# P^T of an attention head rests in DRAM for one head more

## The chip, the core and the metric

The kernel runs on one core of a Trainium2 chip. The core has five engines that work side by side, each with its own queue in order: TensorE (PE; its weight loads are shown apart as PEld), VectorE (DVE), ScalarE (ACT), GpSimd (POOL) and SyncE (SP), which issues all of this kernel's DMAs. The metric is the device time of one execution in microseconds (us). One execution is recorded instruction by instruction: that is the profile.

## The reference

Two transformer layers over 2 batches of 512 rows of 512, all in float32, cut here to what matters:

```python
x = x + layernorm(L0_attn(layernorm(x)))   # 32 heads of 128, 8 of K and V, RoPE, causal
x = x + layernorm(L0_ffn(layernorm(x)))    # one linear layer with LoRA
x = x + layernorm(L1_attn(layernorm(x)))   # 32 heads, RMS norm of q and k, biases, not causal
x = x + layernorm(L1_ffn(layernorm(x)))    # silu(x w1) * (x w3), then w2, with LoRA
# attention: softmax(q k^T / sqrt(128)) v, then a product with Wo
```

Per head the softmax gives a 512 x 512 matrix P. TensorE needs it transposed, P^T, to form O^T = V^T P^T ("P V").

## The kernel before

**Products.** Each float32 operand is split into hi + lo[...], and a product is three matmuls: hi hi, hi lo and lo hi (`mm3`, L393). So most results are read twice: a cast makes hi (ACT, or DVE), a subtraction lo (POOL, or DVE).

**Units and heads.** A unit is two heads of one batch; layer 0 has units 0 to 31, layer 1 units 32 to 63. A head (n, j) is head j of unit n. A unit has projections (q, k, v), scores, softmax, P V and the output projection with Wo (`out_proj`, `post(n)`), which adds to the accumulator y.

**P^T.** In most units ("lag", L1446: units 2 to 26 and 33 to 62) P is transposed in two steps (`softmax_tail`, L681): DVE transposes 32 x 32 blocks into a tile T, a DMA stores T in a DRAM buffer (`pd` in layer 1, `pd0`, shown as pc, in layer 0; three of each, used in turn, L1534), and four DMAs load it back with the blocks in place into a tile PT, by halves of the queries. Then casts and subtractions make the hi and lo tiles "pt" from it, which `av_items` (L839) multiplies with V. In the other units TensorE does the transposes (`pv_items`, L767).

**Order of work.** The program is emitted by a generator on the host which keeps its own estimate of each engine's clock. TensorE's work is a list of items with conditions: a main list in the order of heads and "fills" (projections, output projections, P V), each with a nominal place in main. A fill is issued when its place has come, or earlier when main has to wait (`streams`, L345). The work of other engines follows in stages; a stage is a piece of a Python generator, and `yield` hands over until the time estimated for its work. Each engine then runs its queue in the order emitted. In `run` (L1535 on), the interval of head i holds the scores of head i + 1 and P V of head i - 1.

**Slots.** Large tiles lie in an arena of 37 slots of 4 KB per partition; a tile takes a half or the whole of one (`HALF`, L218). Each kind has a limit of its own, partly different for each of six phases of the work (`PHASES`, L40). Requests for a kind queue in order (`wait`, L325). Weights take W slots: Wq, Wk, Wv and Wo of a unit, or of a pair of units, two slots each in layer 1.

**Scores in layer 1** (`l1_score`, L1169). DVE takes the negative maximum m of each row of the scores from PSUM; a second DVE instruction multiplies m by the row's RMS factor r (mr = m r); ACT computes exp(r s + mr) with two pointer operands.

## Time and profile before

| | us |
|---|---|
| three runs | 2106.71, 2111.2, 2113.66 (median 2111.2) |
| span of the profiled execution | 2117.8 |
| idle of PE in 0 to 110, 590 to 800, 1910 to 2118 | 8.4, 6.0, 11.0 |
| P^T in layer 0 (pc) and layer 1 (pd): first store to last load | 58.0 to 618.6, 817.1 to 1874.0 |
| median from issue to landing: store of T in layer 1, a load of PT, a load of Wo | 3.7, 3.3, 3.6 |

The time of a run is that of the whole execution. The profiled execution is another one and its span is from the first to the last instruction; it is 6.6 us above the median of the runs. Its instructions all carry one line, L102, the helper which records them; they are told apart by their tiles. "ar" is any tile of the arena, "ps_oy" the PSUM bank of P V, of the output projection and of the last feed-forward product, "ps_s" that of the scores, "ps_pj" that of projections, "m", "mr" and "rq" the row values of the scores in layer 1. In a group line the figures are the total busy time, the mean of one instruction, and the engine's idle time just before them with what ended it. In a line of waits they are total, number and longest. In the timeline they are start, length, engine and instruction, with the idle time before it in brackets.

### The profile page before, as it was taken

The page shows a single profiled execution, that of the slowest core. Times are in us where ns is not written, and L with a number is a line of the kernel's source. Part 1 is how long each engine was busy: PE and PEld are TensorE (multiplying, and loading weights), DVE is VectorE, ACT ScalarE, POOL GpSimd, SP SyncE. Part 2 cuts the span into 40 slices and gives each one's busy share as a digit, 9 for nine tenths or more (in the row PEclk, how much of TensorE's full clock was granted, in tenths as well). Part 3 has the DMA queues.
Part 4 walks back from the last instruction along what each step waited for, and adds up shares of the span by engine and source line. Part 5 has one row for each costly group of instructions (what it writes and reads, how often), then busy time and mean ns, then how long its engine had stood idle before and what let it go on. Part 6 is the DMA issues. An engine that isn't in the chain of part 4 may idle for free.

```text
span 2117.8 us, 41211 instructions
## 1 busy us (share of the span) xinstructions
PE 2056.7 (97%) x12605; PEld 1827.5 (86%) x12605; DVE 1801.4 (85%) x4210; ACT 1337.7 (63%) x3247; POOL 1446.3 (68%) x1786
## 2 busy tenths in 40 slices
PE   8999999999999999999999999999999999989998
PEld 7888888888888798889899999999999898977886
DVE  7998899899888889889889999899989988888534
ACT  5776677577766668776666666666667666664212
POOL 5686678688875567877677777777777776774212
PEclk9999999999999999999999999999999999999999
DMA  2476567577652235887877777777777787763021
GB/s 98 127 183 166 145 185 183 143 200 199 177 159 66 71 103 166 244 232 223 227 202 229 220 227 211 207 221 219 225 206 232 213 240 212 224 178 93 31 67 44
DMA packets 476566, 370.54 MB, mean 175 GB/s; under 512 B 117400, under 2 KB 424488, under 8 KB 476344
## 3 DMA queue, kind: packets, MB, share of 16 engines
q1 hardware_dynamic: 476344, 367.91, 60.9%
q8 instruction: 99, 1.62, 0.3%
q14 instruction: 123, 1.01, 0.2%
HBM read 232.12 MB, written 135.66 MB: 174 GB/s over the span
## 4 chain that ended last, share of the span: by engine, by line
PE 54%; DMA 12%; DVE 9%; SPq 3%; issue 2%; POOL 2%; ACT 2%; DVEq 0%; ACTq 0%; POOLq 0%
PE ps_pj L102 23%; PE ps_oy L102 19%; PE ps_s L102 10%; DVE ar L102 6%; SPq L102 3%; DMA pd<-ar 3%; DMA ar<-pd 2%; POOL ar L102 2%; DMA kdk<-ar 2%; ACT ar L102 2%; DMA ar<-kdq 2%; DMA kdq<-ar 2%; PE ps_tr L102 1%; DMA ar<-pc 1%; DVE m L102 1%
## 5 line engine op out<-in xcount | busy, mean ns | idle before, releaser
L102 POOL TENSOR_TENSOR ar<-ar,ar 128x256 fp32r<-128x256 f32 (+4 forms) x1223 | 1058.3, 887 | 456.6 <-ACT ar L102 333.6
L102 PE MATMUL ps_oy<-ar,ar 128*128 128x256 f32 (+2 forms) x4014 | 832.2, 342 | 28.7 <-DVE ar L102 14.0
L102 PEld LDWEIGHTS ps_oy<-ar,ar 128*128 128x128 f32 x4014 | 653.5, 190 | 133.1 <-DVE ar L102 22.5
L102 ACT CAST ar<-ar 128x256 fp32r<-128x256 f32 (+3 forms) x1166 | 531.5, 490 | 305.4 <-DMA ar<-pd 117.1
L102 PE MATMUL ps_pj<-ar,xh 128*128 128x256 f32 (+1 forms) x3392 | 635.2, 285 | 0.9 <-POOL ar L102 0.6
L102 PEld LDWEIGHTS ps_pj<-ar,xh 128*128 128x128 f32 x3392 | 536.0, 190 | 14.5 <-POOL ar L102 1.1
L102 PE MATMUL ps_pj<-ar,xl 128*128 128x256 f32 (+1 forms) x1696 | 482.9, 285 | 0.0
L102 DVE STREAM_TRANSPOSE ar<-ar 128x256 f32<-128x256 f32 (+3 forms) x688 | 347.9, 533 | 16.9 <-DMA pd<-ar 9.7
L102 DVE TENSOR_TENSOR ar<-ps_pj,ar 128x512 f32<-128x512 f32 (+2 forms) x448 | 305.4, 683 | 52.5 <-PE ps_pj L102 44.8
L102 PE MATMUL ps_s<-ar,ar 128*128 128x512 f32 (+2 forms) x1252 | 338.5, 376 | 8.6 <-DVE ar L102 4.7
L102 PEld LDWEIGHTS ps_pj<-ar,xl 128*128 128x128 f32 x1696 | 322.9, 190 | 2.1 <-DVE xl L102 0.7
L102 PE MATMUL ps_pj<-xh,ar 128*128 128x512 f32 x816 | 286.6, 399 | 0.7 <-ACT xh L102 0.7
L102 DVE TENSOR_TENSOR y<-ps_oy,y 128x512 f32<-128x512 f32 x272 | 184.8, 680 | 81.8 <-PE ps_oy L102 80.2
L102 PEld LDWEIGHTS ps_s<-ar,ar 128*128 128x128 f32 x1252 | 214.5, 189 | 44.0 <-DVE ar L102 12.6
L102 DVE TENSOR_TENSOR ar<-ar,ar 128x256 fp32r<-128x256 f32 (+5 forms) x328 | 207.9, 652 | 51.1 <-ACT ar L102 50.1
L102 ACT ACTIVATE ar<-ps_s,mr,rq 128x512 f32<-128x512 f32 x256 | 198.6, 777 | 46.7 <-DVE mr L102 36.9
L102 PEld LDWEIGHTS ps_pj<-xh,ar 128*128 128x128 f32 x816 | 154.0, 189 | 31.7 <-ACT xh L102 1.1
L102 DVE TENSOR_REDUCE m<-ps_s 128x1 f32<-128x512 f32 x256 | 170.9, 673 | 6.2 <-PE ps_s L102 5.0
L102 ACT ACTIVATE ar<-ar,ri 128x512 f32<-128x512 f32 (+3 forms) x245 | 149.6, 621 | 38.3 <-DVE ri L102 37.1
L102 POOL TENSOR_SCALAR ar<-ar,ri 128x512 f32<-128x512 f32 (+3 forms) x202 | 133.0, 661 | 54.3 <-DVE ri L102 48.9
L102 PE MATMUL ps_pj<-xl,ar 128*128 128x512 f32 (+1 forms) x408 | 161.2, 395 | 0.0
L102 ACT ACTIVATE ar<-ps_s,m 128x512 f32<-128x512 f32 (+3 forms) x256 | 133.8, 526 | 23.4 <-DVE m L102 14.8
(91 smaller groups left out, 2105.5 us busy)
## 6 DMA issues: line engine op xcount, KB each, us to landing
pd<-ar SPq DMA_DIRECT2D x240, 256.0 KB, 3.7
ar<-pd SPq DMA_DIRECT2D x480, 128.0 KB, 3.3
ar<-pc SPq DMA_DIRECT2D x200, 128.0 KB, 3.0
ar<-in_wq SPq DMA_DIRECT2D x86, 256.0 KB, 4.1
ar<-in_wo SPq DMA_DIRECT2D x86, 256.0 KB, 3.6
kdk<-ar SPq DMA_DIRECT2D x31, 512.0 KB, 4.8
ar<-kdk SPq DMA_DIRECT2D x124, 128.0 KB, 4.0
kdq<-ar SPq DMA_DIRECT2D x31, 512.0 KB, 5.1
```

The costliest lines, as they stand in the source:

```text
L102: r = self.k.tc.keep_in_program_order(f(*args, **kw))
```

## The change

P V of a lagged head comes two heads behind its scores instead of one: the interval of head i holds P V of head i - 2. With it:

- five DRAM buffers instead of three; a head's store waits in the generator until the head five before it has issued its loads
- in layer 1 the loads, and after them the casts, are issued in the order of heads (`turn`)
- the output projection of a unit moves one head back, and its Wo and V stay that much longer
- tiles of the kinds W, v, nat and raw are given out only while two more slots are free
- the feed-forward weights of layer 1 wait until the last unit's Wo is in
- in layer 1's scores one instruction in place over PSUM multiplies by r and takes the minimum of the row (K carries a negative factor); exp then has the scale -1 and that minimum as its bias
- two stores of x are followed by a `yield` before the tile is released

Without the comments and docstrings that it drops, the diff is:

```diff
@@ room
         free = sum(not u for u in self.used)
+        if tag in ("W", "v", "nat", "raw"):
+            free -= 2
@@ setup
-        self.pd0 = [[...] for i in range(3)]
-        self.pd = [... for i in range(3)]
+        self.pd0 = [[...] for i in range(5)]
+        self.pd = [... for i in range(5)]
+        self.loads, self.turn, self.places = {}, [0, 0], 0
@@ consts
-        ...scalar_tensor_tensor(self.g, self.gqk[:, 0:1], SCALE, ...)
+        ...scalar_tensor_tensor(self.g, self.gqk[:, 0:1], -SCALE, ...)
@@ resid, after each store of x
+            yield
             self.rel(x)
@@ softmax_tail, before T
+        head = st["head", j]
+        while self.loads.get(head - 5, 2) < 2:
+            yield 0.1
+        self.loads.setdefault(head, 0)
@@ softmax_tail, before PT
+        o = 1 - h if st["causal"] else h
+        while not st["causal"] and self.turn[0] < st["place", j] + o:
+            yield 0.1
         yield from self.wait("PT")
+        self.turn[0] = max(self.turn[0], st["place", j] + o + 1)
         (the four loads)
+        self.loads[head] += 1
         yield
+        while not st["causal"] and self.turn[1] < 2 * head + o:
+            yield 0.1
@@ softmax_tail, in the loop over kc, and pv_items with its last transpose
+            if kc == ((0, 1)[h] if st["causal"] else NT - 1):
+                self.turn[1] = max(self.turn[1], 2 * head + o + 1)
@@ l1_score
-            m = self.t("m", [P, 1])
-            nc.vector.tensor_reduce(m, ps, AX.X, ALU.max, negate=True)
-            yield
             while "rq" not in st:
                 yield 0.3
             r = st["rq"][:, 2 * qt + j:2 * qt + j + 1]
-            mr = self.t("mr", [P, 1])
-            nc.vector.tensor_tensor(mr, m, r, ALU.mult)
-            yield
-            self.rel(m)
-            yield from self.softmax_tail(st, j, qt, ps, mr, r, S)
+            m = self.t("m", [P, 1])
+            nc.vector.tensor_scalar(ps, ps, r, 3.0e38, ALU.mult, ALU.min, accum_out=m)
+            yield
+            yield from self.softmax_tail(st, j, qt, ps, m, -1.0, S)
@@ f1_weights, first half of each weight
+                    while "o" not in self.wlast:
+                        yield 0.5
@@ run
+        self.vlast, self.wlast = pre(NA - 1)[2]["v"], wt(NA - 1, 0)
-            pre(n)[2]["slot", j] = i % 3
+            pre(n)[2]["slot", j] = i % 5
+            pre(n)[2]["head", j] = i
+            pre(n)[2]["place", j] = self.places
+            self.places += 2 * lag[n]
+        pend = []
@@ run, j == 0
+                if n > 1 and lag[n - 2] and lag[n - 1]:
+                    fill["o"] += post(n - 2)
@@ run, j == 1
-                if n > 0 and lag[n - 1]:
+                if n and lag[n - 1] and not lag[n]:
                     fill["o"] += post(n - 1)
@@ run, every head
-            if i and lag[heads[i - 1][0]]:
-                todo += av_lag(*heads[i - 1])
+            while pend and (len(pend) >= 2 or not lag[n]):
+                todo += av_lag(*heads[pend.pop(0)])
+            if lag[n]:
+                pend.append(i)
...
-                if L == 0 and i and lag[heads[i - 1][0]]:
+                if L == 0 and lag[n] and todo:
```

More of the change, by code (lines that the diff above doesn't have):

```diff
@@ L416, in setup @@
         self.used = [set() for _ in self.arena]
-        self.pd0 = [[self.dr.tile([P, 4, 2, 64 * (h + 1)], F32, name=f"pc{i}{h}") for h in range(2)] for i in range(3)]
-        self.pd = [self.dr.tile([P, 2, 4, 256], F32, name=f"pd{i}") for i in range(3)]
+        self.pd0 = [[self.dr.tile([P, 4, 2, 64 * (h + 1)], F32, name=f"pc{i}{h}") for h in range(2)] for i in range(5)]
+        self.pd = [self.dr.tile([P, 2, 4, 256], F32, name=f"pd{i}") for i in range(5)]
         self.kd = {n: [self.dr.tile([P, 4, 256], F32, name=f"kd{n}{i}") for i in range(2)] for n in "kq"}
         self.ready = {}
+        self.loads, self.turn, self.places = {}, [0, 0], 0
         self.ident = cp.tile([P, P], F32, name="ident")
@@ L434, in consts @@
         yield
-        nc.vector.scalar_tensor_tensor(self.g, self.gqk[:, 0:1], SCALE, self.gqk[:, 1:2], ALU.mult, ALU.mult)
+        nc.vector.scalar_tensor_tensor(self.g, self.gqk[:, 0:1], -SCALE, self.gqk[:, 1:2], ALU.mult, ALU.mult)
     def bcast(self, tile_, src):
@@ L778, in tr @@
                 self.rel(*[st["p", j, qt] for qt in range(NT)])
+                self.turn[1] = max(self.turn[1], 2 * st["head", j] + 2)
             n = S - q0 * P
@@ L1511, in run @@
         at(f - 1, 1, [self.l1_init])
-        self.vlast = pre(NA - 1)[2]["v"]
+        self.vlast, self.wlast = pre(NA - 1)[2]["v"], wt(NA - 1, 0)
         at(NA - 2, 0, self.f1_init())
@@ L1547, in run @@
                         fill["q"] += qk_mid(n + 1)
-                if lag[n]:
+                if lag[n] and 1:
                     fill["v"] += v_mid(n)
@@ L1553, in run @@
             else:
-                if n > 0 and lag[n - 1]:
+                if n and lag[n - 1] and not lag[n]:
                     fill["o"] += post(n - 1)
+                if lag[n] and 0:
+                    fill["v"] += v_mid(n)
                 if n + 1 < NA and lag[n] and not lag[n + 1]:
```

## The prediction

> **What bounds the kernel now.** First the page's table of busy time:

> ```profile
> PE 2056.7 (97%) x12605; PEld 1827.5 (86%) x12605; DVE 1801.4 (85%) x4210; ACT 1337.7 (63%) x3247; POOL 1446.3 (68%) x1786
> ```

> TensorE is busy for 2056.7 of 2117.8 us. A busy PE need not be at its peak, so I looked at the timeline in mid layer 1: at 1302.80 three matmuls of 256 columns start every 0.36 us, 0.12 each, with no gap. The change alters none of TensorE's work, so what it can win is the 61.1 us of idle time and what hangs on it. The windows by stage say where that lies (columns: length, busy us of PE, PEld, DVE, ACT, POOL, granted clock, DMA share, GB/s):

> ```profile
> 110.00:590.00 480.00, 474.59 (x2601) 414.54 (x2600) 427.46 (x1137) 330.00 (x950) 367.92 (x445) 1.00 0.65 174
> 800.00:1060.00 260.00, 248.82 (x1671) 225.31 (x1672) 228.13 (x501) 187.91 (x425) 195.99 (x239) 0.99 0.76 221
> 1060.00:1700.00 640.00, 634.97 (x4462) 589.19 (x4461) 584.13 (x1295) 417.00 (x961) 479.69 (x579) 1.00 0.76 218
> 1700.00:1850.00 150.00, 143.67 (x976) 133.32 (x975) 123.59 (x281) 99.01 (x225) 108.40 (x130) 0.97 0.79 227
> 1850.00:1910.00 60.00, 52.09 (x289) 43.78 (x288) 53.72 (x116) 41.45 (x85) 42.16 (x58) 0.94 0.60 171
> ```

> Idle in the stages with P^T through DRAM: 5.4 (layer 0), 11.2 (start of layer 1), 5.0 (middle), 6.3 (end) and 7.9 us (tail). The other 25 us (0:110, 590:800, 1910 on) have none or little of it. The waits of PE in these same windows put on ps_oy, the bank of P V and of the output projection, 5.4, 8.4, 0.4, 6.3 and 5.1 us. By form, most of it is at the 256-column matmuls, those of P V:

> ```profile
> L102 PE MATMUL ps_oy<-ar,ar 128*128 128x256 f32 x1932 | 327.8, 287 | 23.7 <-DVE ar L102 9.2 <-POOL ar L102 8.5 <-ACT ar L102 5.6
> ```

> The engines named make hi and lo of P^T. What they wait for stands in the list of waits and in the timeline of one stall:

> ```profile
> ACT ar L102 <- DMA ar<-pd: 117.1, 62, 4.2
> SPq L102 <- DMA pd<-ar: 212.8, 105, 4.7
> ...
> 912.81 1.75 ACT L102 CAST ar<-ar 128x256 fp32r<-128x256 f32 x4 [2.08 <-DMA ar<-pd]
> ...
> 913.26 0.39 PE L102 MATMUL ps_oy<-ar,ar 128*128 128x256 f32 x1 [1.61 <-ACT ar L102]
> ```

> SP waits until P^T has landed in DRAM (212.8 us in all), ACT until it is back (117.1), and PE 1.61 us for ACT. In the chain of waits between 800 and 1060, "DMA pd<-ar" has 10.6% and "DMA ar<-pd" 8.1%. So in the thin places P^T comes late; in the middle of layer 1 TensorE itself is the bound.

> **A. P V one head later.** Its 256-column waits are at most the 20.5 us of ps_oy outside the tail less the 5.1 us of the 512-column form, so 15.4. A head lasts 17 us in layer 1 (the rows of rq are 34 us apart, two heads each), and write and load land in 3.7 and 3.3 us: with a head more, lateness of DRAM is covered. Not covered is the recycling of "pt": a cast still waits for TensorE to release a slot, then costs 402 ns on ACT and 769 on POOL. Bounds 0 and 15.4; I take two thirds, **-10**.

> The clock adds to it:

> ```profile
> 914.20:917.40 3.20, 3.20 (x15) 3.20 (x16) 0.00 (x0) 2.42 (x5) 3.12 (x4) 0.50 0.87 230
> ```

> After the stall of 913 the granted clock is 0.50, and 15 matmuls start where 27 of 0.12 us would: some 1.6 us lost. The same stands at 1023, 1743, 1784 (twice as long), 1876 and 1887. [...] The row decides; two thirds: **-4**.

> What it adds: at the start of each lagged stretch one head's P V is missing, 13 matmuls or some 1.8 us in layer 0 and 24 x 0.12 = 2.9 us in layer 1. Fills drawn forward cover it while weights are there; bounds 0 and 4.7, I take **+1.5**. At the end, heads (62,0), (62,1) and (63,0) all have P V in one head, and the output projection of unit 61 (1859.8 to 1867.5 now) moves a head on. But TensorE has gaps of 0.63 to 1.50 us between 1870 and 1878 that this moved work can fill. Bounds -8.3 (5.1 of waits and two windows of clock) and +10; with DVE at 53.7 of 60 us I take **+3**.

> SP: the same 240 stores and 480 loads; loads wait for PT slots instead of for the landing, so the weights and K^T queued behind them on SP are issued earlier. Nothing charged. The strict order of the casts holds ACT, DVE and POOL stages back in the generator, not in a queue: no cost while a head is in stock. Four more zeroing stores for two more layer-0 buffers fall at unit 1, some 2 us of SP beside a busy PE: 0.

> **B. The scores of layer 1.** DVE now, and the nearest rows for what comes (a pass in place over PSUM, then the read of its accumulator):

> ```profile
> L102 DVE TENSOR_REDUCE m<-ps_s 128x1 f32<-128x512 f32 x256 | 170.9, 673 | 6.2 <-PE ps_s L102 5.0
> L102 DVE TENSOR_TENSOR mr<-m,rq 128x1 f32<-128x1 f32 x256 | 92.2, 365 | 0.0
> L102 DVE CUSTOM_DVE_ANT_0 ps_s<-ps_s,ar 128x512 f32<-128x512 f32 x64 | 44.8, 700 | 0.7 <-PE ps_s L102 0.6
> L102 DVE DVE_READ_ACCUMULATOR2_ANT m<- 128x1 f32 x256 | 35.1, 137 | 0.0
> ```

> 256 x (673 + 365) = 265.7 becomes 256 x (700 + 137) = 214.3 us: 51 us less. The 365 is the doubt: that row goes from 107 to 2451 ns with a median of 218. [...] I take 51. On the path to the end it is little: in the middle of layer 1 DVE has 584 of 640 us, yet PE waits for it only some 5 us. Bounds 0 and -5; **-1**. The exp loses its pointer scale: 777 to 686 ns (layer 0's row), 23 us of an ACT at 63%: 0.

> **C. Slots.** W, v, nat and raw leave two slots free; Wo stays a head longer, as V does. In the middle of layer 1 the Wk load of a pair comes at 1041 and the pow behind its K at 1104, 63 us; I estimate some 43 of them as slack (12 us of projections, 8 of load and split off). Loads 17 us later stay hidden. At the start of layer 1 it is 33 us (787 to 820, 820 to 853), so 13 of slack. **+1**, bounds 0 and +22 (rival 3). FF weights wait for the last Wo: 0, bounds 0 and +20 (rival 2). The yields before a release after a store: 0.

> **Sum.** -10 - 4 + 1.5 + 3 - 1 + 1 = -9.5: a span of 2108.3. Runs stand to this span as 2111.2 to 2117.8 (0.9969), so **2102 us**, 0.45% faster. About 0.3%, 6.3 us, is what a measurement of this kernel tells from no change: faster is below 2104.9, slower above 2117.5.

> **Rivals.**
> 1. *No change.* The waits turn into recycling of "pt" slots, or the order dealt anew puts as many elsewhere. For: at 1871 to 1882 PE waits for P V five times, always for POOL. Against: ACT's 117.1 us on the load. 2110, 0.18.
> 2. *Slower: the FF weights behind the last Wo.* At 1856 FF weights are loaded now; the last Wo follows only at 1897.7 and 1903.0. In the change the former wait for the latter. The first FF matmul is at 1901.1; its weights need 3.0 us to land and 10 from fold (1891.1) to use, Wo 3.6 and some 2 of split. So each us that Wo is issued after 1882 costs one. If it stays where it is, at 1897.7 to 1903, 16 to 21: 2117.8 - 9.5 + 18 = 2126, or **2120**. For: slots W are full there. Against: without the FF weights in line Wo could start with unit 63, at about 1868. 0.22.
> 3. *Slower: weights at the start of layer 1.* With 13 us of slack and 17 of delay, 4 units lose 4 us each and a clock window of 1.6: 22; with the sum 2130, or **2124**. 0.18.

> That the change doesn't do what it says can't be told from order alone; it would look like rival 1.

> **Numbers.** The forecast has 0.42 and a range of its own of 2090 to 2106. Everything won, tail and B's bound included, is about -35, or 2076; that all comes together is unlikely, so the low end is 2082. The high end takes rival 3 with the gain of A halved (+7) and its hole in full (+3.2), 2134. What lies beyond either end is no more than 0.2. Faster 0.42, same 0.18, slower 0.40.

> **What would show it.** Right: ACT's wait for "ar<-pd" below 30 us, SP's for "pd<-ar" well below 100, the 256-column ps_oy idle below 12, no half clock at 914 and 1743, DVE some 50 us less. Wrong: first FF matmul later against the last P V than now (rival 2); PE waiting on ACT casts of in_wk or in_wq between 800 and 950 (rival 3); ps_oy idle as large with POOL as its releaser (rival 1).

## The result and the profile after

The changed kernel is slower by 0.43%: 2120.13 us, median of seven runs (2115.91 to 2125.04), against 2111.2 us of seven runs of the kernel before (2106.71 to 2116.46); ratio 1.0043, 95% interval 1.0025 to 1.006. The forecast was 0.45% faster.

The two profiled executions hide this. A run's time is 1.8 us more than its span (2118.5 for 2116.7 in after). So that of before, with a span of 2117.8, lies above the highest of its seven runs, and that of after in the lower half of its own. Stages are therefore compared here by what PE waits for, not by where a stage ends.

The busy table of after:

```profile
PE 2050.1 (97%) x12605; PEld 1830.9 (86%) x12605; DVE 1755.2 (83%) x4179; ACT 1359.5 (64%) x3315; POOL 1418.6 (67%) x1749
```

Of PE's matmuls, those of 256 columns of the fp32r tiles hi and lo start every 0.12 us; a product of 128 columns of unsplit float32 (`ps_s<-k,q`) is two instructions that start 0.11 us apart. PE's idle time is 66.6 us of the span; it was 61.1. The windows by stage of after (columns as before: length, busy us of PE, PEld, DVE, ACT, POOL, granted clock, DMA share, GB/s):

```profile
110.00:590.00 480.00, 479.81 (x2638) 420.16 (x2637) 426.63 (x1132) 342.62 (x993) 376.61 (x457) 1.00 0.67 178
800.00:1060.00 260.00, 247.89 (x1703) 227.80 (x1702) 224.59 (x514) 188.55 (x426) 203.51 (x247) 0.99 0.80 228
1060.00:1700.00 640.00, 632.34 (x4434) 589.65 (x4433) 550.38 (x1275) 434.61 (x1003) 445.19 (x535) 1.00 0.75 218
1700.00:1850.00 150.00, 141.42 (x964) 129.58 (x963) 129.26 (x293) 97.28 (x222) 112.39 (x136) 0.99 0.81 234
1850.00:1910.00 60.00, 52.41 (x286) 44.65 (x287) 52.65 (x110) 39.97 (x83) 39.73 (x52) 0.94 0.44 137
```

In layer 0 the idle time is gone: 0.2 us of 480 for 5.4. In layer 1 it isn't: 12.1, 7.7, 8.6 and 7.6 us where there were 11.2, 5.0, 6.3 and 7.9. The groups by form say what PE waits for in its place. After:

```profile
L102 PE MATMUL ps_oy<-ar,ar 128*128 128x256 f32 x1932 | 318.5, 286 | 4.2 <-DVE ar L102 2.2 <-POOL ar L102 0.9 <-ACT ar L102 0.7
L102 PE MATMUL ps_s<-ar,ar 128*128 128x512 f32 x901 | 267.5, 403 | 23.1 <-POOL ar L102 8.1 <-DVE ar L102 7.6 <-ACT ar L102 7.0
L102 PE MATMUL ps_tr<-ident,ar 128*128 128x128 f32 x348 | 56.6, 289 | 18.6 <-ACT ar L102 18.3
```

and two rows of before that the prediction did not look at:

```profile
L102 PE MATMUL ps_s<-ar,ar 128*128 128x512 f32 x892 | 269.9, 400 | 8.2 <-DVE ar L102 4.7 <-POOL ar L102 2.2 <-ACT ar L102 1.3
L102 PE MATMUL ps_tr<-ident,ar 128*128 128x128 f32 x348 | 55.6, 285 | 12.3 <-ACT ar L102 11.4 <-DVE xl L102 0.4 <-DVE ar L102 0.2
```

P V's waits fell from 23.7 to 4.2 us. The scores, which read hi and lo of K^T and Q^T, now wait 23.1 us for 8.2; the transposes wait 18.6 for 12.3, and that rise lies mostly in the tail, from 1850 us on. P^T hardly waits for DRAM any more. The waits of SP and ACT in after:

```profile
SPq L102 <- DMA pd<-ar: 70.5, 39, 4.2
...
ACT ar L102 <- DMA ar<-kdq: 27.6, 18, 3.2
...
ACT ar L102 <- DMA ar<-in_wk: 17.5, 9, 4.2
ACT ar L102 <- DMA ar<-kdk: 17.3, 10, 4.4
...
ACT ar L102 <- DMA ar<-pd: 2.9, 1, 2.9
```

The two rows of pd were 212.8 and 117.1. K^T and Q^T (kdk, kdq) take the same kind of way through DRAM. ACT's waits for them in before:

```profile
ACT ar L102 <- DMA ar<-kdq: 8.5, 5, 2.3
ACT ar L102 <- DMA ar<-kdk: 7.5, 6, 2.7
```

With those of DVE and POOL for the same loads, the waits went from 38.1 to 72.3 us. One stall of the scores in after, in the timeline:

```profile
967.46 0.75 DVE L102 TENSOR_SCALAR ar<-ar,g 128x1024 f32<-128x1024 f32 x1 [2.46 <-DMA ar<-kdk]
968.20 0.61 DVE L102 CAST ar<-ar 128x512 fp32r<-128x512 f32 x2
...
969.26 4.23 POOL L102 TENSOR_TENSOR ar<-ar,ar 128x256 fp32r<-128x256 f32 x4
969.33 2.33 DVE L102 TENSOR_TENSOR ar<-ar,ar 128x512 fp32r<-128x512 f32 x2
...
971.71 0.79 PE L102 MATMUL ps_s<-ar,ar 128*128 128x512 f32 x1 [2.17 <-DVE ar L102]
```

K^T lands, DVE scales it by g, casts it, and subtracts for lo until 971.66; POOL meanwhile makes lo of P^T. PE waits 2.17 us. The granted clock falls with it, as it did at 914 in before (window of after, where before has 26 matmuls and a clock of 1.00):

```profile
970.80:974.00 3.20, 2.29 (x5) 1.82 (x6) 3.20 (x5) 1.92 (x4) 3.20 (x4) 0.50 0.72 211
```

In windows of 0.85 us through the whole span, those at half clock before the last 20 us add up to 23.8 us in before and 34.0 in after. By itself that is some 5 us of PE's work, an estimate (half of 10.2). Some 13.6 us of after's 34.0 stand at 28.7, 687.5 and 1947.0, outside the stages in which P^T goes through DRAM; before has its full clock there.

### The profile page after: what moved, and what is told of

The parts are those of the page before. It is cut to its first block, busy times and chain, and to the rows that moved or that the text cites. A ratio compares the mean times of both kernels' runs of the same rounds, so it can differ in the third digit from the quotient of the medians.

```text
span 2116.7 us, 41081 instructions
## 1 busy us (share of the span) xinstructions
PE 2050.1 (97%) x12605; PEld 1830.9 (86%) x12605; DVE 1755.2 (83%) x4179; ACT 1359.5 (64%) x3315; POOL 1418.6 (67%) x1749
## 4 chain that ended last, share of the span: by engine, by line
PE 70%; DMA 9%; DVE 8%; POOL 4%; SPq 3%; issue 3%; ACT 2%; DVEq 0%; POOLq 0%; ACTq 0%
PE ps_pj L102 31%; PE ps_oy L102 24%; PE ps_s L102 13%; DVE ar L102 5%; SPq L102 3%; POOL ar L102 3%; DMA ar<-kdk 3%; PE ps_tr L102 2%; ACT ar L102 2%; DMA ar<-pd 1%; DMA kdq<-ar 1%; DMA pd<-ar 1%; DVE ps_s L102 1%; DMA ar<-pc 1%; DVE y L102 1%
## 5 line engine op out<-in xcount | busy, mean ns | idle before, releaser
L102 POOL TENSOR_TENSOR ar<-ar,ar 128x256 fp32r<-128x256 f32 (+3 forms) x1234 | 1065.0, 888 | 418.4 <-ACT ar L102 302.4
L102 PE MATMUL ps_oy<-ar,ar 128*128 128x512 f32 (+2 forms) x4014 | 824.9, 341 | 8.0 <-DVE ar L102 5.8
L102 PEld LDWEIGHTS ps_oy<-ar,ar 128*128 128x128 f32 x4014 | 656.2, 190 | 103.4 <-DVE ar L102 10.2
L102 ACT CAST ar<-ar 128x256 fp32r<-128x256 f32 (+3 forms) x1169 | 532.9, 489 | 212.1 <-PE ps_oy L102 73.2
L102 PE MATMUL ps_pj<-ar,xh 128*128 128x256 f32 (+1 forms) x3392 | 633.6, 285 | 0.0
L102 PEld LDWEIGHTS ps_pj<-ar,xh 128*128 128x128 f32 x3392 | 535.4, 190 | 12.8
L102 PE MATMUL ps_pj<-ar,xl 128*128 128x256 f32 (+1 forms) x1696 | 482.7, 285 | 0.9 <-DVE xl L102 0.9
L102 DVE TENSOR_TENSOR ar<-ps_pj,ar 128x512 f32<-128x512 f32 (+2 forms) x448 | 307.1, 686 | 92.0 <-PE ps_pj L102 82.0
L102 ACT ACTIVATE ar<-ps_s,m 128x512 f32<-128x512 f32 (+3 forms) x512 | 309.3, 606 | 99.8 <-DVE ps_s L102 53.6
L102 PE MATMUL ps_s<-ar,ar 128*128 128x512 f32 (+2 forms) x1271 | 337.1, 377 | 23.6 <-POOL ar L102 8.1
L102 DVE STREAM_TRANSPOSE ar<-ar 128x256 f32<-128x256 f32 (+3 forms) x688 | 347.3, 534 | 12.6 <-DMA pd<-ar 5.6
L102 PEld LDWEIGHTS ps_pj<-ar,xl 128*128 128x128 f32 x1696 | 322.5, 190 | 2.7 <-DVE xl L102 1.3
L102 PE MATMUL ps_pj<-xh,ar 128*128 128x512 f32 x816 | 287.6, 400 | 1.1 <-ACT xh L102 1.1
L102 PEld LDWEIGHTS ps_s<-ar,ar 128*128 128x128 f32 x1271 | 219.0, 190 | 58.3 <-POOL ar L102 12.5
L102 DVE TENSOR_TENSOR ar<-ar,ar 128x256 fp32r<-128x256 f32 (+3 forms) x322 | 215.5, 681 | 47.7 <-ACT ar L102 44.9
L102 DVE TENSOR_TENSOR y<-ps_oy,y 128x512 f32<-128x512 f32 x272 | 185.0, 681 | 81.8 <-PE ps_oy L102 79.3
L102 ACT ACTIVATE ar<-ar,ri 128x512 f32<-128x512 f32 (+3 forms) x287 | 178.1, 630 | 40.8 <-DVE ri L102 39.9
L102 POOL TENSOR_SCALAR ar<-ar,ri 128x512 f32<-128x512 f32 (+3 forms) x189 | 127.3, 675 | 113.1 <-DVE ri L102 86.5
L102 DVE TENSOR_SCALAR_CACHE_REDUCE ps_s<-ps_s,rq 128x512 f32<-128x512 f32 x256 | 188.8, 742 | 16.9 <-PE ps_s L102 15.4
L102 PEld LDWEIGHTS ps_pj<-xh,ar 128*128 128x128 f32 x816 | 153.0, 188 | 31.9 <-ACT xh L102 1.7
L102 PE MATMUL ps_pj<-xl,ar 128*128 128x512 f32 (+1 forms) x408 | 160.5, 393 | 0.5 <-DVE xl L102 0.5
L102 DVE CUSTOM_DVE_ANT_0 ps_s<-ps_s,ar 128x512 f32<-128x512 f32 (+3 forms) x256 | 121.9, 488 | 7.4 <-PE ps_s L102 7.3
```

The costliest lines, as they stand in the source:

```text
L102: r = self.k.tc.keep_in_program_order(f(*args, **kw))
```

## The experiments

A ratio is to the kernel before, run in turn with it on the same chip, with its 95% interval. Three theories were on record first. **1**: the scores now wait for K^T and Q^T on their way through DRAM. **2**: the ends of the lagged stretches cost. **3**: the new score instructions cost, by what they do or by the order that is dealt with them. The first four runs led to **4**: each edit makes the generator deal the order of all work anew, and before's order is a better one than those dealt since.

### Parts of the change alone

score_only is before with the new scores; lag_only the change with the old scores; lag_l0 and lag_l1 have P V two heads behind in one layer, one head behind in the other:

```diff
-            while pend and (len(pend) >= 2 or not lag[n]):
+            while pend and (len(pend) >= (2, 1)[L] or not lag[n]):   # lag_l0; (1, 2) in lag_l1
-                if n > 1 and lag[n - 2] and lag[n - 1]:
+                if (2, 1)[L] == 2 and n > 1 and lag[n - 2] and lag[n - 1]:
-                if n and lag[n - 1] and not lag[n]:
+                if n and lag[n - 1] and (not lag[n] or (2, 1)[L] == 1):
```

> The kernel before with the new scores of layer 1 alone (one pass in place with the factor and the minimum). Theory 1 (the scores now wait for K^T and Q^T, because P V one head later takes the place in front of them): the lag is to blame, so this is 0.998 to 1.000 of before, some 2100 to 2111 us, with DVE about 40 us less busy. Theory 2 (the ends of the lagged stretches cost more than the middle wins): the same, 0.998 to 1.000. Theory 3 (the new scores cost, by what they do or by the order dealt anew): 1.004 or more.

> The changed kernel with the old scores of layer 1. Theories 1 and 2: 1.004 or a little more (2120 to 2125 us); idle of the 256-column P V matmuls below 8 us as in the change. Theory 3: below 1.000, about 2102 us as forecast.

> The changed kernel with two heads of lag in layer 0 alone, one head in layer 1. Theory 1 (K^T and Q^T go through DRAM in layer 1 only): 0.997 to 1.000, since layer 0 keeps its gain of 5 us and layer 1 has its P V waits back but not the new score waits. Theory 2: 1.002 to 1.004, with the loss between 590 and 800 us.

> The changed kernel with two heads of lag in layer 1 alone, one head in layer 0. Theory 1: 1.004 to 1.007, score waits above 20 us. Theory 2: 1.001 to 1.003, the loss from 1850 us on.

Measured: score_only 1.0058 (1.0043 to 1.0073), lag_only 1.017 (1.0157 to 1.0183), lag_l0 1.0039 (1.0026 to 1.0052), lag_l1 1.0097 (1.0084 to 1.011). No theory holds: the scores alone are slower, the lag alone is slower still, and both together are 1.0043. Effects that do not add say that the edits act on each other, or that something else changes with every edit. Two more expectations failed: lag_only's 256-column P V waits are 16.7 us, not below 8, and lag_l1's scores wait 16.9 us, not above 20.

### The same instructions in the same order

new_in_old_order has the new score instructions, but the generator goes on counting the old ones' time, so that the order on every engine is that of before but for the scores' own. old_in_new_order is the reverse, in after's order. The core of the first:

```diff
-            nc.vector.tensor_reduce(m, ps, AX.X, ALU.max, negate=True)
+            nc.vector.raw("tensor_scalar", ps, ps, r, 3.0e38, ALU.mult, ALU.min, accum_out=x)
+            nc.vector.tick("tensor_reduce", x, ps, AX.X, ALU.max, negate=True)
```

Here `raw` issues without touching the generator's clocks and `tick` moves the clocks without issuing; the second DVE instruction and the scale of exp are treated alike.

> The kernel before with the new score instructions in the place of the old ones, while the generator goes on counting the old ones' time: every engine's order is that of before, instruction by instruction, but for the scores' own. Theory 4 (the effects do not add because each edit lets the generator deal the whole order anew, and before's order is a better one than those dealt since): what made the scores alone 1.0058 is the order, so here 0.995 to 1.000. Rival (Theory 3: the new score instruction costs by what it does, holding its bank and DVE 880 ns in one piece): as before's order cannot have changed, 1.004 to 1.007 as with the scores alone. DVE some 45 us less in both.

> The changed kernel with the old score instructions put back, every engine's order that of after but for the scores' own. Theory 4: the old instructions add some 45 us of DVE and 23 of ACT to an order dealt for less, so 1.005 to 1.010, and the 1.017 of the two-head lag with the old scores was mostly its own deal. Rival: the two-head lag as such needs the relief of DVE, then it comes near 1.017 here too (1.014 to 1.020).

Measured: 0.9997 (0.9985 to 1.0009) and 1.0108 (1.0089 to 1.0127). The new instructions cost nothing in before's order, so score_only's 0.58% is its order. In after's order they are worth 0.65%. Their rows in new_in_old_order:

```profile
L124 DVE TENSOR_SCALAR_CACHE_REDUCE ps_s<-ps_s,rq 128x512 f32<-128x512 f32 x256 | 189.2, 745 | 11.9 <-PE ps_s L102 10.9
...
L124 DVE DVE_READ_ACCUMULATOR ps_s<-ps_s,rq 128x1 f32 x256 | 36.1, 141 | 0.0
```

225.3 us of DVE for 263.1, and nothing of it reaches the end: in this order DVE's time is free, as step B said.

### Nothing changed but the deal

One number of the generator, its estimate of the delay from one engine to the next, is changed; the kernel computes the same with the same rules. What is dealt anew is the order and, with it, which engine gets a cast or a subtraction (ACT has 3247 instructions in before, 3309 with 0.11).

```diff
-LAT = 0.1
+LAT = 0.09
```

> The kernel before with nothing changed but one number of the generator, its estimate of the delay between engines (0.09 us for 0.1): the same work, the same rules, an order dealt anew. Theory 4: outside of 1.000 by 0.3% or more, most likely slower, 1.003 to 1.012. Rival (the order dealt anew is worth nothing, the edits cost by what they do): 0.998 to 1.002.

> As the one before, with 0.11 us for 0.1. Theory 4: 1.003 to 1.012, and not the same as with 0.09. Rival: 0.998 to 1.002.

> The changed kernel with the generator's estimate of the delay between engines at 0.09 us for 0.1: its work and its rules, an order dealt anew. Theory 4 (the order dealt is worth more than the edits): not at after's 1.0043, anywhere from 1.000 to 1.015. If the two-head lag and the new scores together are a gain under an order that is not picked, it stands below the kernel before with the same number (1.0107); if the lag costs by itself, at or above it. Rival (the edits cost by what they do): 1.002 to 1.006.

> As the one before with 0.11 us; to be set beside the kernel before with 0.11 (1.0153). Theory 4: 1.000 to 1.015, and below 1.0153 if the edits are a gain. Rival: 1.002 to 1.006.

lag_none is the changed kernel with P V one head behind (as in lag_l0 and lag_l1, in both layers); it was run with all three numbers too.

> The changed kernel with P V one head behind its scores as before; the new scores, the two slots held free, the order of loads and the wait of the feed-forward weights stay. Theory 4: a deal of its own, 1.003 to 1.012. Theory 2 (the lag costs at the ends of its stretches): below after, 0.996 to 1.002.

> The changed kernel with P V one head behind as before, and the generator's delay at 0.09 us: beside after_lat09 (1.0186) it differs in the lag alone. If the lag gains what the wait for P^T was worth, 1.021 to 1.026; if the lag by itself costs, 1.008 to 1.015; if the order dealt hides either, anywhere from 1.003 to 1.020.

> As the one before with 0.11 us, beside after_lat11 (1.0103). If the lag gains, 1.013 to 1.018; if it costs, 1.000 to 1.007; if the order dealt hides either, anywhere from 1.003 to 1.020.

| ratio (interval) | 0.1 | 0.09 | 0.11 |
|---|---|---|---|
| before | 1 | 1.0107 (1.0088 to 1.0125) | 1.0153 (1.0133 to 1.0172) |
| changed | 1.0043 (1.0025 to 1.006) | 1.0186 (1.0169 to 1.0203) | 1.0103 (1.0086 to 1.0121) |
| changed, P V one head behind | 1.007 (1.0054 to 1.0086) | 1.0112 (1.0093 to 1.013) | 1.0072 (1.0057 to 1.0087) |

**An order dealt anew costs more than the change.** A hundredth of a microsecond in one estimate makes the kernel before 1.07% or 1.53% slower, the second beyond the 0.3 to 1.2% expected; after_lat09, with 1.0186, lies beyond the 1.015 expected of it. The waits of before with 0.11 are of the same kinds as after's:

```profile
L102 PE MATMUL ps_s<-ar,ar 128*128 128x512 f32 x903 | 273.4, 409 | 24.0 <-DVE ar L102 15.5 <-POOL ar L102 5.3 <-ACT ar L102 3.0
```

The last two rows of the table differ in the lag alone. The lag makes -0.27%, +0.74% and +0.31%: the sign of its worth cannot be told from three such deals. But what it does to the waits has the same sign in all three pairs (idle of PE in us before the 256-column matmuls into ps_oy, before all forms into ps_s, and in all):

| | P V, 256 columns | scores | all of PE |
|---|---|---|---|
| 0.1: one head, two heads | 17.9, 4.2 | 12.1, 25.4 | 60.9, 66.6 |
| 0.09 | 18.0, 13.5 | 12.9, 23.8 | 72.5, 83.8 |
| 0.11 | 19.0, 12.1 | 15.8, 27.1 | 67.9, 75.8 |

With the numbers of 0.11, one head behind first, then two:

```profile
L102 PE MATMUL ps_oy<-ar,ar 128*128 128x256 f32 x1932 | 326.2, 285 | 19.0 <-POOL ar L102 12.0 <-DVE ar L102 5.3 <-ACT ar L102 0.9
L102 PE MATMUL ps_s<-ar,ar 128*128 128x512 f32 x929 | 273.2, 402 | 14.8 <-ACT ar L102 9.4 <-POOL ar L102 4.0 <-DVE ar L102 1.0
```

```profile
L102 PE MATMUL ps_oy<-ar,ar 128*128 128x256 f32 x1932 | 319.0, 286 | 12.1 <-POOL ar L102 8.1 <-ACT ar L102 2.0 <-DVE ar L102 1.9
L102 PE MATMUL ps_s<-ar,ar 128*128 128x512 f32 x903 | 275.1, 405 | 26.4 <-DVE ar L102 13.8 <-POOL ar L102 6.3 <-ACT ar L102 6.2
```

Each time the lag takes 5 to 14 us of waits from P V and puts 11 to 13 at the scores, and PE's idle time in all is 6 to 11 us longer. The other kernels with two heads of lag in both layers have long waits at the scores too: 28.9 us in lag_only (with 16.7 at P V) and 25.7 in no_gate. lag_l1, with two heads in layer 1 alone, has only 16.9. So in the three pairs the exchange of waits goes with the lag, though an order alone can bring such waits (24.0 us above).

### The wait for the stores priced at a fixed order

The loads of P^T (p_early) or of K^T and Q^T in layer 1 (k_early) read a weight in HBM, in the same shape, in place of the buffer that was stored; so they wait for no store. They keep their place in SP's queue and still take their time to land, and the trace shows them under the weight's name, in_wk. The order on every engine stays; what is multiplied is not P, or not k and q.

```diff
-            nc.sync.dma_start(pt[32 * b:32 * b + 32, :, :n], d[:, b, :].rearrange("(a k) c -> k a c", a=4))
+            nc.sync.dma_start(pt[32 * b:32 * b + 32, :, :n],
+                              self.a["wk1"][h, :, b, :n].rearrange("(a k) c -> k a c", a=4))
```

> The kernel before, its order unchanged on every engine; the loads of P^T read a weight in HBM in the same shape in place of the buffer that P was stored in, so they wait for no store (what is multiplied with V is not P). It prices the wait for P^T that the change is to hide. Step A of the prediction (waits 10, clock 4): 0.992 to 0.995. Rival (those waits are mostly the recycling of pt and of engines, or what follows is late as well): 0.998 to 1.001.

> The same in the changed kernel, order unchanged. If a head more covers DRAM fully, nothing is left to win: 1.003 to 1.006, as after (1.0043). If P^T still comes late somewhere or its loads hold up SP's queue: below 1.001.

> The kernel before, order unchanged, with the loads of K^T and Q^T in layer 1 reading a weight in HBM in place of the buffers they were stored in (so the scores are not those of q and k). Waits on scores are 8.2 us here: 0.995 to 0.999.

> The same in the changed kernel, order unchanged. Theory 1 (the wait for P^T became a wait for K^T and Q^T on their way through DRAM, 23.1 us at the scores and the half clock after some of them): 0.990 to 0.997, a gain of 15 to 30 us on after. Rival (they are late by the work on DVE, ACT and POOL, not by DRAM): 1.001 to 1.005.

| | P^T early | K^T and Q^T early |
|---|---|---|
| before (1) | 0.9947 (0.9934 to 0.996) | 1.0 (0.9986 to 1.0013) |
| changed (1.0043) | 1.0025 (1.0014 to 1.0036) | 1.0027 (1.0016 to 1.0037) |

In before's order the wait for the stores of P^T is worth 2113.17 - 2101.15 = 12.0 us (8.5 to 13.9 by the interval). SP's wait for "pd<-ar" falls from 212.8 to 12.8 us. ACT still waits 121.1 us for in_wk, which now holds the loads of P^T in both layers; in before it waited 170.4 for pd, pc and in_wk together. So the 12 us are the price of the stores, not of the loads. The groups and the window of the stall at 914, in before with P^T early:

```profile
L102 PE MATMUL ps_oy<-ar,ar 128*128 128x256 f32 x1932 | 325.7, 286 | 15.5 <-POOL ar L102 6.8 <-DVE ar L102 4.5 <-ACT ar L102 3.6
```

```profile
914.20:917.40 3.20, 3.20 (x22) 2.88 (x21) 3.20 (x7) 1.76 (x5) 3.20 (x5) 1.00 0.86 229
```

8 us of waits are gone, and the clock is whole there (22 matmuls for 15); the half-clock windows fall from 23.8 to 10.2 us. In the changed kernel no gain from the same step can be told (1.0025 beside 1.0043, the intervals overlap). Nor does the kernel before gain anything with K^T and Q^T early (1.0, where 0.995 to 0.999 was expected). In the changed kernel that makes 1.0027, where theory 1 expected 0.990 to 0.997, and the scores still wait:

```profile
L102 PE MATMUL ps_s<-ar,ar 128*128 128x512 f32 x901 | 269.3, 406 | 19.0 <-DVE ar L102 7.3 <-ACT ar L102 6.3 <-POOL ar L102 5.3
```

ACT's wait for those loads has not gone; it has changed its name:

```profile
ACT ar L102 <- DMA ar<-in_wk: 58.7, 36, 4.5
```

In after in_wk, kdk and kdq together are 62.4 us (17.5, 17.3 and 27.6). So the stores of K^T and Q^T are not most of what the scores wait for: without them 19.0 of the 23.1 us stay. Whether it is the loads, or when they are issued and the engines come to make hi and lo, this run does not say; theory 1 stays open in that part.

### The wait of the feed-forward weights for Wo

no_gate takes these lines out of the change:

```diff
-                    while "o" not in self.wlast:
-                        yield 0.5
```

> The changed kernel without the wait of the layer-1 feed-forward weights for the last Wo; the order can differ only where those weights are loaded, the last 260 us. If the wait costs (the rival of the prediction with the weights behind the last Wo), 1.000 to 1.003; if it costs nothing, 1.003 to 1.006; if it guards Wo, above 1.007, with the last Wo near 1900 us again.

Measured: 1.0027 (1.0017 to 1.0037). The last Wo is loaded at 1895.8 then, for 1855.7, and the first feed-forward matmul stands at 1895.3 in both. 1.0027 lies in the range expected for a wait that costs, but the difference to 1.0043, 0.16%, is not separated from nothing by the intervals. The waits do differ: without these lines the 128-column transposes wait 10.8 us for 18.6 (12.3 in before), so their rise goes with this wait or with the order that it deals.

## Why the prediction was wrong

**A, the waits of P V and the clock (-14): of the right size, at a fixed order.** before_p_early measures 12.0 us for the two terms together, from the stores alone. All the signs named came: ACT's wait for ar<-pd 2.9 us, SP's for pd<-ar 70.5, P V's idle 4.2, no half clock at 914 and 1743, DVE 46 us less busy. In the change P V's waits fell by 19.5 us, twice the 10 assumed; the early loads take away 8.2 of them, and what took the rest, the later P V or the order, is not separated. No run shows the -4 of the clock by itself: before_p_early has it together with the waits, and there the half-clock windows fall from 23.8 to 10.2 us. The 1.61 us of stall before 913.26 came with a half-clock window, and without the stall it was gone (0.50 and 1.00 from 914.20 to 917.40). That before_p_early's 2101 us is almost the 2102 forecast is chance: it has none of the other terms.

**B, the scores (-1 on the path): right at before's order, mis-sized for DVE.** The pass took 742 ns and its accumulator 138 in after, 880 for the 837 assumed, so 256 x (1038 - 880) = 40 us of DVE and not 51; on the path nothing (0.9997). At before's order all of DVE is 32.6 us less busy (1801.4 to 1768.8). Why the old multiply took 365 ns in the mean, from 107 to 2451, no run shows. In after's order the same instructions are worth 0.65%, beyond the bounds of 0 and -5 us: the old ones add 43 us of DVE and 25 of ACT to an order dealt without them.

**A, what it adds (+4.5): not contradicted.** PE idles 12.1 us for 11.2 from 800 to 1060, 7.6 for 7.9 from 1850 to 1910, and 13.8 for 10.8 after it. These are net of what the change won there, so the term stands by itself in no run.

**C, slots and the gate (+1): no fault seen.** PE has no idle time at its projections between 800 and 1060, and the wait of the feed-forward weights is worth 0.16%, not told from nothing (no_gate); their first matmul comes at 1895.3, for 1901.1 in before.

**The step that failed is the sum.** It took away waits and left all else where it stood: it had no term for new waits of TensorE at the scores (11 to 13 us in the three pairs) and none for an order dealt anew (24 and 33 us for before's own work). First, **what is late next**: the prediction named only the recycling of "pt", and priced the move of the output projection in the tail alone. In the steady part of layer 1 that move takes the output projection out of the interval in which K and Q of a later unit are projected. Read off the traces, as medians over units 35 to 61 (the stages of K^T by DVE's sums of squares, SP's store and loads, the scaling by g, and DVE's first pass over the scores):

| us | before | lag_none | lag_none_lat11 | after | after_lat11 |
|---|---|---|---|---|---|
| first pass of head 0 to that of head 1 | 16.1 | 18.0 | 17.4 | 12.5 | 15.7 |
| head 1 to head 0 of the next unit | 18.4 | 16.7 | 17.6 | 21.9 | 21.0 |
| K's first sum to its second | 8.4 | 7.8 | 8.3 | 4.1 | 3.6 |
| second sum to K^T scaled by g | 19.6 | 18.6 | 18.0 | 22.6 | 22.1 |
| K^T scaled to first pass of its scores | 7.6 | 8.5 | 8.9 | 5.6 | 5.9 |

The intervals of the two heads become unequal, K's chain from its second sum to K^T takes 3 to 4 us longer, and K^T is ready 2 to 3 us closer to its scores. In nine traces with one head of lag in layer 1 the last row lies between 7.4 and 10.0, in six with two heads between 5.1 and 7.5. The exception among the six is after_lat09, with 7.5: its intervals are 15.6 and 18.7, its chain takes 19.5 where kernels with one head have 17.4 to 19.6, and its scores wait 23.8 us all the same. lag_l1 has 5.1 us in the last row and waits 16.9 at the scores, before_lat11 has 8.1 and waits 24.4. So the shift comes with the lag in five of six traces, but it does not tell how long the scores wait. That the moved output projection makes the shift is argued from the intervals; it was not run by itself.

Second, **the order dealt anew**. Rival 1 had it in half a sentence, as a way for the gain to come to nothing, with 0.18. It is larger than the change itself: before's own work takes 1.07% and 1.53% longer in two other orders, and every order dealt since lies 0.27% to 1.9% above before's. Why before's is a good one, by luck or by choice, no run shows. The case for faster, 0.42, had no room for that.

From before to after, then, PE's waits fell by 19.5 us at P V and rose by 14.9 at the scores and 6.3 at the transposes; with the smaller rows its idle time is 5.5 us up. These two executions cannot carry the +9 measured, for PE's busy time is 6.6 us down (2056.7 to 2050.1). A shorter execution in before's order is that of before_k_early (ratio 1.0): a span of 2108.6, idle 57.9, busy 2050.7. Beside it after is 8.1 us longer, 8.7 more of idle time and 0.6 less of busy time. On that reading the loss is PE's waits, and its longer half clock does not show as busy time. How much of the loss belongs to the lag and how much to this order stays open: three pairs put the lag at -0.3% to +0.7%.

No kernel that computes the reference beat the one before; new_in_old_order equals it.

## What to carry to other kernels

Where a program emits the order of work from its own estimates, an edit changes every queue, not only its own part: first jog an estimate that means nothing and see what that costs, then price the edit at a frozen order (issue the new instruction, count the old one's time) or over several deals. A wait that is hidden need not be won, if the next input of the same engine has no slack: list the chains that end at TensorE (here P^T, and K^T and Q^T) with the slack of each before one is given a head more. The wait for a store can be priced at a fixed order, by a load of the same shape from a tensor that nothing writes; the load's own time stays, under another name in the trace.

## What the hardware showed unexpectedly

And a pass in place over PSUM that also accumulates is two instructions on DVE, 742 ns and 138 ns for 128x512, 69 ns more than the plain row maximum (673) with its single result.
